# Row numbers of keys written by ScalarE, four blocks of tiles instead of three, and another order of the quantile units, in a two-layer graph kernel

## The chip, the cores and the metric

The kernel runs on one core of a Trainium2 chip. The metric is the device time of one execution in microseconds (us), the median of the runs. Engine names: PE is the matrix engine (PEld its weight loads), DVE the vector engine, ACT the scalar engine, POOL the GpSimd engine, SP the engine that only starts transfers. SBUF is the working memory of 128 partitions; PSUM is the small memory that PE writes. DRAM is the chip's large memory.

## The reference, cut to what matters

`x` is 4096 nodes by 128 numbers, `adj` a 4096 by 4096 matrix of zeros and ones with about 32 ones in a row (11 to 55 in this input). Two layers follow each other:

```python
# layer 0: graph attention with 8 heads over the neighbours of each node
Wh = einsum('nd,hde->hne', nodes, W)
e  = leaky_relu(f1[:, :, None] + f2[:, None, :], 0.2)
att = softmax(where(adj > 0, e, -9e15))
cat = elu(einsum('hnm,hmd->hnd', att, Wh)) as (N, H*D)
x1  = layernorm(nodes + elu(cat @ W1 + b1))
# layer 1: drop some neighbours of each row, then for each column
# the 0.25, 0.5 and 0.75 quantile of the kept neighbours' x1
keep = mask & ~((rank + 1) % skip == 0)
svals = sort(where(keep, x1[neighbour], big))
agg   = mean over q of svals[ceil(q * n_keep) - 1]
out   = (0.5 * agg + 0.5 * x1) @ W.T + b + x1
```

Rows with few neighbours make both layers sparse: the kernel works on lists of neighbours.

## The kernel before, in words

A *tile* is 128 nodes; there are 32. The work has three stages, and each engine runs its instructions in the order in which the program emits them (`manual_schedule(engines=ORDERED)` for PE, DVE, ACT and POOL; only SP's transfers are ordered by the compiler).

**Search** (`neighbours`). For each tile, ACT reads half a row block of `adj` (`adj_t`, 1 MB) and writes its signs as bf16 (`sgn`, L645). For each of 8 chunks of 512 columns, PE makes a *key* in PSUM in two matmuls: L684 multiplies `sgn` by 8192 times the identity (start of the sum), and L687 adds the column's number, counted down from 4096, from two constant rows (`parts`). DVE takes the 8 largest keys of each 128 columns (L651, four of them per chunk), and then eight passes of L656 and L658 over those pick the neighbours of the tile before. Keys lie in a pool `key_ps` of two PSUM buffers. One chunk of this is a *piece*; `pieces_of(n)` counts them. `complete_records` (L724 to L759) makes the lists final, and `rank_by_count` ranks the nodes of a block by their number of neighbours, so that a tile of the attention holds nodes with lists of like length. POOL scatters the records in that order (`rec_d`, L228).

**Attention** (`step`, `fetch_rows`, `attend`). The tiles are split into `BLOCKS = [6, 10, 16]`: block b is searched while block b - 1 is attended, and the first block is searched before any attention, with the node products of `node_rows` in between. `CAPS` and `LAYERS` give how many list places a tile of a block has; each place costs one gather of 128 rows (L219, `G<-xt_d,idx`), 1124 in all. A `step` fetches tile i on POOL, runs the first part of `attend` on tile i - 1 and the second part on tile i - 2, and strews a quota of search pieces between them. Gathered rows lie in 6 buffers `G` of 16 places, which come free when PE's matmuls L1015 (`y<-wide,G`) have read them. Four PSUM tiles serve the attention: `small` (sums `den`, and the output `o` of L1046), `rz`, `y` and `hT`. The last tile of a block waits for the ranks: its gathers are mixed with the record scatters of the next block. During the last block records go out once more for all nodes (`all_d`), and `lists_of_layer_1` makes the lists of layer 1.

**Quantiles** (`quantile_out`). The 32 tiles are now ranked over all nodes and form 21 units, eleven of them pairs of tiles: `[0]`, `[1]`, `[2, 3]` ... `[22, 23]`, `[24]` ... `[31]`, the last with the longest lists (62 gathers; `[0]` and `[1]` have 22 each). POOL gathers a unit's rows into `vals`, a pool of two buffers (L219, `vals<-x_d,idx`); DVE runs a selection network on it (`tensor_tensor` minimum and maximum, L1228). Between these `turn_of_gpsimd` puts a tiny copy (L1199, `junk<-still`) whenever 1.1 us or more of them have run. PE and ACT then form the output (L1246 to L1273), and POOL scatters it (`out_dram`, L228). The order was `[0]`, `[24]` ... `[31]`, the pairs from the last to the first, `[1]`. The emitted order on POOL is: the fetches of the first two units, and then for each further unit its fetch, followed by the output scatter of the unit two before it. A fetch into `vals` has to wait until the network of the unit two before it has read that buffer.

If a bound on the lists were broken, a flag would start a general path (`general_attention`, `general_quantiles`) behind the three stages.

Of the kernel before, what the change touches and what calls it, by code (L numbers as in the profile page):

```python
# [9 lines left out]
F32 = mybir.dt.float32  # L10
# [9 lines left out]
P = 128  # L20
# [12 lines left out]
MARK = 8192.0  # L33
ROUNDS = L // 8
GROUP = 4
STEPS = 24
KEEP_MIN = 6.0
FMAX = 30.0
# [3 lines left out]


CAPS = {
    6: [28, 30, 33, 35, 39, 61],
    10: [26, 28, 30, 31, 33, 34, 36, 38, 40, 61],
    16: [24, 26, 28, 29, 30, 31, 31, 32, 33, 34, 35, 36, 38, 39, 42, 62],
    32: [
        23, 24, 25, 26, 27, 27, 28, 29, 29, 30, 30, 30, 31, 31, 32, 32,
        33, 33, 34, 34, 35, 35, 36, 36, 37, 37, 38, 39, 40, 41, 44, 63,  # L50
    ],
}
BLOCKS = [6, 10, 16]


LAYERS = {
    (6, 0): [(0, 16, 0), (16, 8, 0), (24, 4, 1)],
    (6, 2): [(0, 32, 0), (32, 8, 7)],
    (6, 5): [(0, 32, 0), (32, 16, 0), (48, 16, 15)],
    (10, 0): [(0, 16, 0), (16, 8, 0), (24, 4, 2)],  # L60
    (10, 4): [(0, 32, 0), (32, 32, 31)],
    (10, 7): [(0, 32, 0), (32, 4, 0), (36, 4, 2)],
    (10, 9): [(0, 32, 0), (32, 16, 0), (48, 16, 14)],
    (16, 14): [(0, 32, 0), (32, 8, 0), (40, 4, 2)],
    (16, 15): [(0, 32, 0), (32, 16, 0), (48, 16, 14)],
}


TURNS = {6: range(6), 10: range(10), 16: [0, 1, 2, 3, 15, 4, 5, 6, *range(8, 15), 7]}

CAP = CAPS[NT]
LOW = [
# [6 lines left out]
for _u in UNITS:  # L79
    for _t in _u:  # L80
        HT[_t] = max((CAP[t] - 1) // 2 for t in _u)
LMAX = 2 * max(HT)
SLOTS = max(2 * HT[u[0]] * len(u) for u in UNITS)


# [157 lines left out]
def kernel(  # L243
# [48 lines left out]
    before = rp.tile([P, P], BF16, name="before")  # L292
    adjp = tc.alloc_tile_pool(name="adjp", bufs=2, side="right")
    cp = tc.alloc_tile_pool(name="cnt", bufs=2, side="right")
    kp = tc.alloc_tile_pool(name="key_ps", bufs=2, space=PSUM)
    parts = [adjp.tile([64, n], BF16, name=f"parts{n}", bufs=1) for n in (N // 8, 7 * N // 8)]
    markb = adjp.tile([P, P], BF16, name="markb", bufs=1)
    rowi = adjp.tile([P, P], F32, name="rowi", bufs=1)

    def search(t0, n):  # L300
        return neighbours(
            tc, adjp, cp, kp, rec, num, adj, t0, n, parts, markb, oneb, bad, jp1, pidx
        )

    with tc.tile_pool(name="setup", bufs=1) as sp, tc.tile_pool(
        name="setup_ps", bufs=2, space=PSUM
    ) as pp, tc.manual_schedule(engines=ORDERED):

        for v in parts:
            nc.vector.memset(v, 0.0)  # L310
        nc.vector.memset(oneb, 1.0)
        for v, base in zip(parts, (N, N - N // 8)):
            n = v.shape[1] // 64
            iota(nc, v[0:1, :], [[-64, n], [0, 64]], base=base)
            iota(nc, v[32:33, :], [[0, n], [-1, 64]])
        nc.vector.tensor_scalar(markb, ident, MARK, None, ALU.mult)
        iota(nc, pidx, [[0, 1]], cm=1)
        iota(nc, jp1, [[1, L]], base=1)
        nc.gpsimd.iota(
            rec.bitcast(I32)[:, :, R_OWN], pattern=[[P, NT]], base=0, channel_multiplier=1  # L320
        )
        iota(nc, rowi, [[1, P]])
        rows = node_rows(tc, sp, pp, rec, x, W, W_sb, a1, a2, Wl, wa, WlT, ident, bad, xt_d)
        for i, _ in enumerate(search(0, BLOCKS[0])):
            if i > 0:
                next(rows, None)
        for _ in rows:
            pass
        nc.vector.tensor_scalar(before, rowi, pidx, None, ALU.is_gt)
        nc.sync.dma_start(W1_sb, W1.rearrange("(h e) o -> e h o", e=P))  # L330
        for i, v in enumerate((b1, gamma, beta, bl)):
            nc.sync.dma_start(vecs[:, i, :], v.partition_broadcast(P))
        for i, big in enumerate((-BIG, BIG)):
            fill = sp.tile([P, D], F32, name=f"fill{i}")
            nc.gpsimd.memset(fill, big)
            nc.sync.dma_start(x1_d[N + i * P : N + (i + 1) * P, :], fill)
# [5 lines left out]

    weigh, store, tail = [], [], []
    consts = {}
    consts["small"] = pp.tile([P, 512], F32, name="small")

    narrow = {
        w: attp.tile([P, 32 // w, NARROW[w]], F32, name=f"narrow{w}", bufs=1) for w in NARROW
# [145 lines left out]


    pairs = [u for u in UNITS if len(u) == 2]
    order = UNITS[:1] + UNITS[2 + len(pairs) :] + pairs[::-1] + UNITS[1:2]
    with tc.tile_pool(name="sort", bufs=2) as sp, tc.tile_pool(name="fin", bufs=3) as fp, tc.tile_pool(
        name="fin_ps", bufs=2, space=PSUM
    ) as pp, tc.manual_schedule(engines=ORDERED):  # L500
        halfid = sp.tile([P, P], F32, name="halfid", bufs=1)
        nc.scalar.mul(halfid, ident, 0.5)
        still = pp.tile([P, 1], F32, name="still", bufs=1)
        nc.vector.memset(still, 0.0)
        late = dict(ident=ident, halfid=halfid, ones=ones, WlT=WlT, bl_b=vecs[:, 3, :], still=still)

        def fetch_unit(unit):
            n, k = 2 * HT[unit[0]], len(unit)
            vals = sp.tile([P, SLOTS * D], F32, name="vals")
            xs = fp.tile([P, 2, D], F32, name="xs")  # L510
            for j in range(n):
                for u, t in enumerate(unit):
                    a = (j * k + u) * D
                    gather(nc, vals[:, a : a + D], x1_d, idx[:, t, j : j + 1])
            for u, t in enumerate(unit):
                gather(nc, xs[:, u, :], x1_d, own_i[:, t : t + 1])
            return unit, vals, xs

        def write_out(unit, o):
            for u, t in enumerate(unit):  # L520
                scatter(nc, out, o[:, u, :], own_i[:, t : t + 1])

        fetched = fetch_unit(order[0])
        done = None
        for nxt in order[1:] + [None]:
            now = fetched
            if nxt:
                fetched = fetch_unit(nxt)
            if done:
                write_out(*done)  # L530
            done = quantile_out(tc, sp, fp, pp, *now, wt, late)
        write_out(*done)
    keep.release()

# [89 lines left out]
    return ROUNDS * (n + 1) + 3 * len(groups_of(n))  # L624


def neighbours(tc, adjp, cp, kp, rec, num, adj, t0, n, parts, markb, oneb, bad, jp1, pidx):


    nc = tc.nc  # L630
# [30 lines left out]
    for t in range(t0, t0 + n):  # L661
        cnt = adjp.tile([P, 2], F32, name="cnt", bufs=20)
        todo += [(t, 0, cnt), (t, 1, cnt)]
        counts[t] = cnt
    for _ in range(3):
        load()
    sign()
    late = None
    start = t0
    for t in range(t0, t0 + n + 1):  # L670

        if t < t0 + n:
            first = adjp.tile([P, NCH * 8], F32, name="first")
            firsts.append(first)
        for r in range(ROUNDS):
            done = late
            late = None
            if t < t0 + n:
                b = r % (ROUNDS // 2)
                if b == 0:  # L680
                    sgn = signs.pop(0)

                key = kp.tile([P, 512], F32, name="key")
                nc.tensor.matmul(  # L684
                    key, lhsT=markb, rhs=sgn[:, ts(b, 512)], start=True, stop=False
                )
                nc.tensor.matmul(  # L687
                    key, lhsT=oneb[0:64, :], rhs=parts[1][:, ts(r - 1, 512)] if r else parts[0], start=False, stop=True
                )
                late = (key, first, r * 512)  # L690
                if b == 0:
                    sign()
            if done:
                eights(*done)
            if t > t0:
                best(firsts[-2 if t < t0 + n else -1], t - 1, r)
            yield
        if t > t0:
            u = t - 1
            cnt = counts[u]  # L700
            nc.vector.tensor_tensor(num[:, u : u + 1], cnt[:, 0:1], cnt[:, 1:2], ALU.add)
            nc.vector.tensor_scalar(rec[:, u, 0:L], rec[:, u, 0:L], -MARK, 0.0, ALU.add, ALU.max)
            if t - t0 in groups_of(n):
                yield from complete_records(tc, cp, rec, num, bad, jp1, pidx, start, t - start)
                start = t
# [232 lines left out]
def attend(tc, ap, pp, fetched, consts):  # L938
# [20 lines left out]
    nc.scalar.activation(zs, zs, AF.Exp)  # L959
    yield  # L960

    small = consts["small"]
    den = small[:, 0 : 32 * H]
    for i, (w, g0, runs, f1v) in enumerate(parts):
        k = P // w
        for r in range(k // 4):
# [9 lines left out]
    rden = ap.tile([4, 32 * H], F32, name="rden", bufs=1)  # L976
    nc.vector.tensor_scalar(rden, den[0:4, :], TINY, None, ALU.max)
    nc.vector.reciprocal(rden, rden)  # L978
    rz = pp.tile([P, L * H], F32, name="rz")
    for i, (w, g0, runs, f1v) in enumerate(parts):  # L980
        k = P // w
        for r in range(k // 4):
# [58 lines left out]
    yield  # L1041
    nc.vector.tensor_scalar(hf, hf, 1.0, -1.0, ALU.min, ALU.add)
    nc.vector.tensor_tensor(hf, hT, hf, ALU.max)  # L1043
    o = small[:, 32 * H : 32 * H + D]
    for h in range(H):
        nc.tensor.matmul(  # L1046
            o, lhsT=hv[:, h, :], rhs=consts["W1_sb"][:, h, :], start=(h == 0), stop=(h == H - 1)
# [120 lines left out]
    nc.vector.tensor_copy(total, tot)  # L1168


def quantile_out(tc, sp, fp, pp, unit, vals, xs, wt, late):

    nc = tc.nc
    k = len(unit)
# [26 lines left out]
    for r, (d, mins, maxs) in enumerate(network):  # L1201
        after = list(where)
        for low, slots, op in ((0, mins, ALU.min), (d, maxs, ALU.max)):
# [4 lines left out]
            for (_, _, at), same in kinds.items():  # L1208
# [5 lines left out]
                parts = list(parts)  # L1214
                while parts:
                    i, c, s, m = parts.pop(0)
                    if then(c * m) > TURN_MAX:
                        room = int((TURN_AIM - then(0)) / (size * TT_EACH))
                        if ran and room < 1:
                            turn_of_gpsimd()  # L1220
# [11 lines left out]
                        op,  # L1232
                    )
                    ran = then(c * m)
                    if ran > TURN_MIN:
                        turn_of_gpsimd()
                        ran = 0.0
                for i in same:
# [262 lines left out]
```

## Time and profile before

| what | value |
|---|---|
| median of 3 runs | 3558.73 us (3556.36 to 3559.92) |
| the profiled execution's own time | 3561.78 us |
| its span in the profile | 3560.0 us |
| busy: PE, DVE, ACT, POOL | 1257.6, 2700.2, 403.2, 2510.0 us |
| first attention gather starts | 137.69 us |
| last attention gather starts | 1768.53 us |
| first quantile gather starts | 1818.31 us |
| last quantile gather starts (`xs`) | 3481.76 us |

A line of a group in the profile reads: line of the kernel, engine, operation, output and inputs, count; then busy time and mean duration of one in ns; then the engine's idle time just ahead of these instructions and what ended most of it ("issue": nothing that the profile shows). A line of the timeline reads: start, duration, engine, line, operation, and in brackets the idle time before it with what ended it. A line of waits reads: who waited, for whom, total us, times, the longest. A window line reads: from and to, its length, and for each engine the busy us and, behind an x, the number of instructions.

### The profile page before, as it was taken

To read this page: it belongs to the slowest core of one execution; us is meant where nothing else is said; L and a number is where in the kernel's file an instruction comes from. 1 tells how busy PE (TensorE), PEld (TensorE's weight loads), DVE (VectorE), ACT (ScalarE), POOL (GpSimd) and SP (SyncE) were. 2 spreads that over 40 slices of the span, in tenths; PEclk is the share of its full clock that TensorE was granted. 3 is DMA by queue.
4 is the path that set the end of the run, shared out by engine and by line. 5 is a ranking of instruction groups with operands and counts; after the bars stand their busy time and mean duration, and the time that the engine had idled before them with its cause. 6 is when DMAs were issued, how large, how long until landed. Compare 5 with 4: busy or idle time off the path is not lost. (4 is left out here: it accounts for less than half of the span.)

```text
span 3560.0 us, 22296 instructions
## 1 busy us (share of the span) xinstructions
PE 1257.6 (35%) x5323; PEld 949.8 (27%) x5323; DVE 2700.2 (76%) x7015; ACT 403.2 (11%) x579; POOL 2510.0 (71%) x2341
## 2 busy tenths in 40 slices
PE   7377568878555454555620000000000000000101
PEld 2144545555455454454520000000000000000101
DVE  8787458877435222247538999999999999999998
ACT  3122122222111111111110000000000000000000
POOL 1475767657777777777747777788777688777771
PEclk9955556555556555555555555555555555555555
DMA  6442254432222222232211111111111111111110
GB/s 232 136 150 77 67 159 131 139 119 75 59 65 54 56 53 55 54 70 55 52 30 48 47 46 46 43 43 41 44 42 46 34 40 41 41 42 41 40 42 12
DMA packets 109132, 237.42 MB, mean 67 GB/s; under 512 B 46720, under 2 KB 63104, under 8 KB 100800
## 3 DMA queue, kind: packets, MB, share of 16 engines
q0 software_dynamic: 74368, 156.34, 17.6%
q10 hardware_dynamic: 14848, 70.85, 5.8%
q1 hardware_dynamic: 19776, 8.73, 1.2%
q8 instruction: 44, 0.72, 0.1%
q14 instruction: 96, 0.79, 0.1%
HBM read 224.60 MB, written 11.15 MB: 66 GB/s over the span
## 5 line engine op out<-in xcount | busy, mean ns | idle before, releaser
L219 POOL DMA_INDIRECT vals<-x_d,idx x1024 | 1219.8, 1191 | 315.7 <-issue 308.7
L219 POOL DMA_INDIRECT G<-xt_d,idx x1124 | 1094.5, 974 | 419.9 <-issue 330.8
L1228 DVE TENSOR_TENSOR work<-work 128x512 f32<-128x512 f32 (+7 forms) x1194 | 933.7, 811 | 0.6
L1247 PE MATMUL st_ps<-dg,goal 128*128 128x128 f32 x286 | 71.4, 427 | 1605.9 <-DVE goal L1228 1605.1
L1228 DVE TENSOR_TENSOR work<-work,work 128x512 f32<-128x512 f32 (+6 forms) x821 | 590.8, 741 | 0.5
L1015 PE MATMUL y<-wide,G 128*128 128x32 f32 (+3 forms) x2248 | 485.6, 394 | 29.0 <-DVE wide L1002 28.9
L1247 PEld LDWEIGHTS st_ps<-dg,goal 128*128 128x128 f32 x286 | 63.3, 322 | 1612.3 <-issue 1611.4
L1015 PEld LDWEIGHTS y<-wide,G 128*128 128x128 f32 x2248 | 463.5, 310 | 65.4 <-DVE wide L1002 31.8
L651 DVE MAX8 first<-key 128x8 f32<-128x128 f32 x1024 | 225.2, 282 | 109.0 <-PE key L687 108.6
L952 DVE TENSOR_TENSOR z<-G,f1x 128x128 f32<-128x128 f32 (+5 forms) x92 | 28.8, 327 | 307.7 <-DMA G<-xt_d,idx 302.3
L684 PE MATMUL key<-sgn,markb 128*128 128x512 bf16 x256 | 150.5, 588 | 131.8 <-DVE first L651 87.9
L1228 DVE TENSOR_TENSOR work<-vals 128x1536 f32<-128x1536 f32 (+7 forms) x96 | 133.4, 1404 | 47.9 <-DMA vals<-x_d,idx 47.5
L1199 DVE COPY junk<-still 128x1 f32<-128x1 f32 x1118 | 168.8, 151 | 0.0
L645 ACT ACTIVATE sgn<-adj_t 128x2048 bf16<-128x2048 int32 x64 | 122.1, 1907 | 333.8 <-PE key L684 277.9
L1046 PE MATMUL small<-W_sb,late 128*128 128x128 f32 x512 | 127.3, 434 | 88.3 <-DVE late L1043 88.3
L1246 ACT ACTIVATE dg<-ident,wt 128x128 f32<-128x128 f32 x143 | 47.5, 394 | 930.9 <-PE st_ps L1247 930.6
L967 PE MATMUL small<-z,own 128*4 128x32 f32 (+6 forms) x438 | 49.3, 279 | 285.4 <-ACT z L959 285.4
L687 PE MATMUL key<-parts,oneb 64*128 64x512 bf16 x256 | 148.4, 580 | 0.5 <-POOL parts L237 0.5
L1046 PEld LDWEIGHTS small<-W_sb,late 128*128 128x128 f32 x512 | 112.8, 327 | 102.6 <-DVE late L1043 98.9
L983 PE MATMUL rz<-rden,ownT 4*128 4x32 f32 (+6 forms) x438 | 96.6, 383 | 78.6 <-DVE rden L978 63.7
L1034 PE MATMUL hT<-late,W_sb 128*128 128x128 f32 x512 | 110.2, 383 | 35.4 <-ACT late L1028 35.4
L228 POOL DMA_INDIRECT out_dram<-o,own_i x32 | 44.7, 1398 | 105.9 <-ACT o L1273 83.6
(184 smaller groups left out, 1784.4 us busy)
## 6 DMA issues: line engine op xcount, KB each, us to landing
adj_t<-in_adj_dram ACTq DMA_DIRECT2D x64, 1024.0 KB
G<-xt_d,idx POOLq DMA_INDIRECT x1124
vals<-x_d,idx POOLq DMA_INDIRECT x1024
R<-rec_d SPq DMA_DIRECT2D x128, 26.2 KB
xt_d<-rec SPq DMA_DIRECT2D x4, 544.0 KB
rec<-in_x_dram ACTq DMA_DIRECT2D x4, 512.0 KB
narrow<-rec_d SPq DMA_DIRECT2D x68, 5.2 KB
a_b<-in_L_gnn_a_dram ACTq DMA_DIRECT2D x2, 512.0 KB
```

Source lines behind the costliest of these rows:

```text
L219: nc.gpsimd.indirect_dma_start(out=dst, out_offset=None, in_=rows, in_offset=bass.IndirectOffsetOnAxis(ap=idx, axis=0),)
L645: nc.scalar.activation(sgn, adj_t, AF.Sign, accum_out=cnt[:, i : i + 1])
L651: nc.vector.max(first[:, ts(c0 // CW + c, 8)], key[:, ts(c, CW)])
L684: nc.tensor.matmul(key, lhsT=markb, rhs=sgn[:, ts(b, 512)], start=True, stop=False)
L687: nc.tensor.matmul(key, lhsT=oneb[0:64, :], rhs=parts[1][:, ts(r - 1, 512)] if r else parts[0], start=False, stop=True)
L983: nc.tensor.matmul(rz[:, layer[i] * H : (layer[i] + w - g0) * H], lhsT=ownT[w][:, r, :], rhs=rden.rearrange("p (g r h) -> p r g h", r=k // ...
L1015: nc.tensor.matmul(yf[:, ts(g, c)], lhsT=G[:, col + j - a, 0:D], rhs=pf[:, ts(j, c)], start=(i == 0 and g % (w // 2) == w // 2 - 1), stop= ...
L1034: nc.tensor.matmul(hT[:, ts(h, P)], lhsT=consts["W_sb"][:, h, :], rhs=yT[:, h, :], start=True, stop=True)
L1046: nc.tensor.matmul(o, lhsT=hv[:, h, :], rhs=consts["W1_sb"][:, h, :], start=(h == 0), stop=(h == H - 1))
L1199: nc.vector.tensor_copy(junk, late["still"])
L1228: nc.vector.tensor_tensor(slots_of(dst, (j, c, s, m), size), slots_of(a, (i, c, s, m), size), slots_of(b, (i + d, c, s, m), size), op,)
L1247: nc.tensor.matmul(st_ps[:, u, :], lhsT=goal[:, (j * k + u) * D : (j * k + u + 1) * D], rhs=dg, start=(j == 0), stop=False,)
```

## The change

It has five parts.

1. The column numbers of keys no longer come from PE. ACT writes them into the PSUM buffer (`seed`: an Identity activation of a constant row `rows` with the chunk's `base` as bias, 128x512), and the one matmul that is left adds onto them (`start=False`). A buffer's first use in a search is opened by a matmul with `start=True`. There are three key buffers instead of two, and a seed is issued two chunks ahead of its matmul. `parts` and its set-up are gone.
2. `small` is gone, which frees the PSUM bank for the third key buffer: `den` lies in `rz`, and `o` in the first 128 columns of `hT`.
3. `BLOCKS = [4, 6, 9, 13]`, with `CAPS`, `LAYERS` and `TURNS` of their own. The list places are 151 + 217 + 317 + 451 = 1136 gathers, where 217 + 351 + 556 = 1124 were.
4. The units' order is `[0]`, `[1]`, `[24]` ... `[30]`, the pairs from the last to the first, `[31]`. Units `[0]` and `[1]` share one `vals` buffer, and the fetches of the first three units stand in a row. POOL's order of fetches and output scatters keeps its form.
5. The last unit (`[31]`) runs its network without `turn_of_gpsimd` and without cutting long instructions.

```diff
+KEYS = 3
-BLOCKS = [6, 10, 16]
+BLOCKS = [4, 6, 9, 13]
...
-    kp = tc.alloc_tile_pool(name="key_ps", bufs=2, space=PSUM)
-    parts = [adjp.tile([64, n], BF16, name=f"parts{n}", bufs=1) for n in (N // 8, 7 * N // 8)]
+    kp = tc.alloc_tile_pool(name="key_ps", bufs=3, space=PSUM)
+    rows = adjp.tile([P, 512], F32, name="rows", bufs=1)
+    base = adjp.tile([P, ROUNDS], F32, name="base", bufs=1)
...
-        for v in parts:
-            nc.vector.memset(v, 0.0)
         nc.vector.memset(oneb, 1.0)
-        for v, base in zip(parts, (N, N - N // 8)):
-            n = v.shape[1] // 64
-            iota(nc, v[0:1, :], [[-64, n], [0, 64]], base=base)
-            iota(nc, v[32:33, :], [[0, n], [-1, 64]])
+        iota(nc, rows, [[-1, 512]])
+        iota(nc, base, [[-512, ROUNDS]], base=N)
...
+    def seed(r):
+        key = kp.tile([P, 512], F32, name="key")
+        if len(opened) < KEYS:
+            nc.tensor.matmul(key, lhsT=markb, rhs=signs[0][:, 0:512], start=True, stop=True)
+            opened.append(key)
+        nc.scalar.activation(key, rows, AF.Identity, bias=base[:, r : r + 1])
+        seeded.append(key)
+
     for _ in range(3):
         load()
     sign()
+    opened, seeded = [], []
+    chunks = [r for _ in range(n) for r in range(ROUNDS)]
+    for _ in range(KEYS - 1):
+        seed(chunks.pop(0))
...
-                key = kp.tile([P, 512], F32, name="key")
-                nc.tensor.matmul(
-                    key, lhsT=markb, rhs=sgn[:, ts(b, 512)], start=True, stop=False
-                )
-                nc.tensor.matmul(
-                    key, lhsT=oneb[0:64, :], rhs=parts[1][:, ts(r - 1, 512)] if r else parts[0], start=False, stop=True
-                )
+                key = seeded.pop(0)
+                nc.tensor.matmul(
+                    key,
+                    lhsT=markb,
+                    rhs=sgn[:, ts(b, 512)],
+                    start=False,
+                    stop=True,
+                    skip_group_check=True,
+                )
...
             if done:
                 eights(*done)
+            if chunks:
+                seed(chunks.pop(0))
...
-    small = consts["small"]
-    den = small[:, 0 : 32 * H]
+    rz = pp.tile([P, L * H], F32, name="rz")
+    den = rz[:, 0 : 32 * H]
...
-    o = small[:, 32 * H : 32 * H + D]
+    o = hT[:, 0:D]
...
-    order = UNITS[:1] + UNITS[2 + len(pairs) :] + pairs[::-1] + UNITS[1:2]
+    alone = UNITS[2 + len(pairs) :]
+    order = UNITS[:2] + alone[:-1] + pairs[::-1] + alone[-1:]
...
-            vals = sp.tile([P, SLOTS * D], F32, name="vals")
+            if unit is order[1]:
+                vals = shared[0][:, SHORT * D : (SHORT + n) * D]
+            else:
+                vals = sp.tile([P, SLOTS * D], F32, name="vals")
+                shared.append(vals)
...
-        fetched = fetch_unit(order[0])
+        fetched = [fetch_unit(v) for v in order[:2]]
         done = None
-        for nxt in order[1:] + [None]:
-            now = fetched
-            if nxt:
-                fetched = fetch_unit(nxt)
+        for i in range(len(order)):
             if done:
                 write_out(*done)
-            done = quantile_out(tc, sp, fp, pp, *now, wt, late)
+            if i + 2 < len(order):
+                fetched.append(fetch_unit(order[i + 2]))
+            now, last = fetched.pop(0), i == len(order) - 1
+            done = quantile_out(tc, sp, fp, pp, *now, wt, late, last)
...
-                    if then(c * m) > TURN_MAX:
+                    if not last and then(c * m) > TURN_MAX:
...
-                    if ran > TURN_MIN:
+                    if not last and ran > TURN_MIN:
                         turn_of_gpsimd()
```

## The prediction

> **What bounds the kernel now.** I read the page first (slices and costliest groups), then POOL's timeline for the ends of the stages, then the waits and windows inside the attention, then windows that count gathers and turns in the sorts.
>
> The page, the 40 slices (89 us each) and four groups:
>
> ```profile
> DVE  8787458877435222247538999999999999999998
> POOL 1475767657777777777747777788777688777771
> ...
> L219 POOL DMA_INDIRECT vals<-x_d,idx x1024 | 1219.8, 1191 | 315.7 <-issue 308.7
> L219 POOL DMA_INDIRECT G<-xt_d,idx x1124 | 1094.5, 974 | 419.9 <-issue 330.8
> ...
> L684 PE MATMUL key<-sgn,markb 128*128 128x512 bf16 x256 | 150.5, 588 | 131.8 <-DVE first L651 87.9
> ...
> L687 PE MATMUL key<-parts,oneb 64*128 64x512 bf16 x256 | 148.4, 580 | 0.5 <-POOL parts L237 0.5
> ```
>
> Three stages show. In slices 1 and 2 POOL does next to nothing while DVE searches. From 137.69 to 1769.5 us (last gather's end) POOL gathers nearly without a break: 7 tenths is full here, since a gather of 0.974 us is followed by 0.30 of issue, 1.274 in all. From slice 22 DVE sorts at 9 tenths, and POOL is near full beside it. POOL's waits from 137 to 1770 us, DVE's from 463 to 925, and all engines in that window:
>
> ```profile
> POOL G L219 <- PE y L1015: 73.3, 8, 30.0
> ...
> POOL x_d L228 <- DVE f1b L898: 7.4, 1, 7.4
> ```
>
> ```profile
> DVE first L651 <- PE key L687: 72.5, 44, 4.8
> ```
>
> ```profile
> 463.00:925.00 462.00, 369.11 (x1471) 244.52 (x1471) 354.18 (x1312) 120.36 (x128) 314.98 (x323) 0.59 0.40 117
> ```
>
> So while a block is searched the attention falls behind the gathers: POOL waits for `G` buffers (73.3 us), because DVE waits for keys (72.5 us of 462) behind a PE that is busy for 369.1 us; ACT is busy for 120.4.
>
> In the sorts, the start of the first two units and the pace of POOL (windows of units `[24]`, `[31]` and `[6, 7]`; first the gathers L219, then the turns L1199):
>
> ```profile
> 1847.17 1.83 DVE L1228 TENSOR_TENSOR work<-vals 128x768 f32<-128x768 f32 x2 [32.05 <-DMA vals<-x_d,idx]
> 1897.90 1.29 DVE L1228 TENSOR_TENSOR work<-vals 128x512 f32<-128x512 f32 x2 [15.49 <-DMA vals<-x_d,idx]
> ```
>
> ```profile
> 1897.90:1963.00 65.10, 49.76 (x47) 0.50 0.18 48
> 2395.30:2539.50 144.20, 115.06 (x92) 0.51 0.16 42
> ...
> 3293.30:3374.80 81.50, 62.91 (x49) 0.52 0.15 40
> ```
>
> ```profile
> 1897.90:1963.00 65.10, 6.86 (x46) 0.50 0.18 48
> 2395.30:2539.50 144.20, 14.41 (x96) 0.51 0.16 42
> ...
> 3293.30:3374.80 81.50, 7.62 (x51) 0.52 0.15 40
> ```
>
> 47 gathers against 46 turns, 92 against 96, 49 against 51: beside a sort POOL gets about one gather for each turn, every 1.4 to 1.6 us. That is what the new order of units has to live with.
>
> **Part 1, the first search.** One tile takes DVE 12.6 us (L701 starts at 80.13 and at 92.75), and the first block's record scatters follow each other every 2.8 us (114.80 to 128.69, five steps). Two tiles fewer: 25.2 + 5.6, and about 1 for shorter ranks: 32 us, first gather at 106. Three covers. ACT: per tile two signs of 2.1 with 0.7 of transfer issue, eight copies of 0.26, two of 0.21, and eight seeds. A seed's price lies between copies from PSUM of 128x256 (0.37 us) and the Exp of 128x1024 (1.02); by their slope 0.59, so 4.7 in all. The sum, 12.1, still lies under DVE's 12.6; at 1.02 a seed ACT would take 15.5 and cost 3 us a tile, 12 in all. `node_rows` gets 42 search pieces to hide behind where it had 61, so some ten of its steps run after them, 0.55 us each (copies at 61.10, 61.63, 62.17) on PE and ACT; they hide behind DVE's last eight-passes (9.8 us from 92.86 on), and cost 6 if not. The opening matmuls are 12 of 0.59 us on PE, which waits anyway.
>
> **Part 2, POOL's work in the attention.** Before: 1124 x 1.274 = 1432, 86 scatters between the gathers at about 1.3 = 112, and pauses. POOL's timeline gives pauses of 22.3, 8.0 and 30.0 us in the steps, and 18.0 and 6.8 around the two block changes (lists must land, and a tile of 49 or 50 places takes four buffers): 85 in all. 1432 + 112 + 85 = 1629; it took 1631.8. After: 1136 x 1.274 = 1447 (+15), 88 scatters (two more record scatters) = 114, and the same rest of 3: 106 + 1564 = 1670 plus pauses. Three block changes at 12.4 (mean of the two): 37.
>
> **Part 3, the pauses in the steps.** Before, 60.3 us over 14 steps with search pieces (5 + 9), 4.3 each. Now there are 3 + 5 + 8 = 16 steps, with as much search in each (6/3, 9/5, 13/8 tiles against 10/5, 16/9). A step of the second block took 462/9 = 51 us, in which PE was busy 41 and DVE waited 8.1 for keys. With 14.2 chunks a step PE loses 14.2 x 0.54 (two keys start 0.54 apart) = 7.7 us, and a third buffer lets it run one chunk (1.6 us of DVE) further ahead. Bounds: all 8.1 go, a step (43) is shorter than the fetch of a tile (36 gathers, 47 us), and no pause is left; or nothing goes, because the seed of 0.59 stands in the chain from DVE's read to the next key where L687's 0.54 stood, and ACT in its order may hold it behind a sign (2.1), the copy L1028 (1.88) and table loads (1.28): 16 x 4.3 = 69. Only the matmuls' share is sure, so I take half, 4 us a step; as the fetch then sets the pace of some steps, 1.8 of pause is left: 29. Last gather at 1670 + 37 + 29 = 1736, **34 us earlier** (63 earlier with no pause, 6 later with all). The way from there to the first quantile gather (48.8 us) holds one tile's attention, unchanged. `den` in `rz` and `o` in `hT` wait for reads of the tile before that DVE has long done; nothing.
>
> **Part 4, the order of units.** At the start nothing is won: `[0]` sorts for 35.2 us while the next fetch took 50.7 (the 15.5 of idle above). Now `[0]` and `[1]` sort for 35.2 + 32.1 while two fetches (23 + 37 transfers at 1.37) take 82: idle 15 again. The end is what changes. Before, POOL took 1664 us from 1818.3 to its last fetch, 21 of them idle (6.5 and 14.8, waiting for an output): 1643 of work, 92 gathers of it during `[31]`'s 144.2 us. As `[31]` now sorts last, all fetches must be done before that sort begins. Their work is the same 1643, less about 12, since some 40 gathers run at 1.24 beside an idle DVE instead of 1.5: 1631 after the first gather. DVE alone would be there earlier: 29 + 35 + 32 + 15 + 1472 (its sorts from 1897.9 to 3546.5 without `[31]` and `[1]`) = 1583. So DVE waits 48 us more; adding the fetches and sorts up unit by unit puts 35 of them ahead of `[31]`, the rest ahead of the last pairs.
>
> **Part 5, the last unit without turns.** 96 turns of 0.07 us (start to start) go: 144 becomes 137. 1631 + 137 = 1768 against 1728 before (3546.5 less 1818.3): 40 later. Behind the sort PE has 14 targets instead of 4, and about nine matmul pairs of 0.5 us come after the last minimum instead of four: 3 more. With 1 for the landing, **44 us later**. Bounds: at 3% off the pace of the gathers, 20 to 70; if POOL kept up, 4 earlier (7 less 3).
>
> **Sum.** 3561.8 (the profiled execution) - 34 + 44 = 3572; the median lay 3 under that execution: **3569 us**.
>
> **A rule against part 1.** No row of before has ACT writing into a buffer that PE then adds to. The Trainium skill, "PSUM — Partial Sum Buffer", section "The four PSUM rules", says that ScalarE's writes neither set nor clear the bits that make a matmul add, and that a seed other than 0 is safe only where an earlier matmul left the bit set. By it the opening matmuls are what makes the seeds count, and without them every list would be wrong; the sum would then be the general path's, not mine.
>
> **Rivals.** (a) *Key waits vanish*: no pauses, -63 + 44 = -19, 3540, faster. It decides when a step gets shorter than a tile's fetch, 47 us. For it: PE's 369 of 462. Against: the waits on PE's own chains stay. 0.22. (b) *The fetches keep up*: -34 - 4, 3521. Against: one gather a turn in every window. 0.08. (c) *ACT takes PE's place* in the chain: +6 + 44, 3609. 0.15. (d) *The seeds don't add*: lists wrong, the flag starts the general path, thousands of us. 0.02. My forecast: 0.53, by itself 3552 to 3586.
>
> **How the numbers follow.** This kernel can be told from no change at about 0.2%, 7 us. Of the forecast 0.31 lies above, 0.15 within, 0.07 below; (a) gives 0.20 and 0.02, (b) 0.08 below, (c) and (d) 0.17 above. Rounded: faster 0.34, same 0.17, slower 0.49. The range reaches from (a)'s to near (c)'s time: 3536 to 3604.
>
> **What would show it.** First gather at 106; DVE's waits for keys under 4.5 us a step; last `G` gather near 1736; idle of DVE ahead of `[31]`'s first L1228 about 35 us, with POOL gathering `vals` back to back until then. Wrong, if `[31]` starts without a wait, or if the `G` waits for `y` are above 70 or near 0.

## The result, and the profile after

The changed kernel takes 3552.7 us (median of 20 runs, 3548.4 to 3558.9), the kernel before 3557.9 in as many. The ratio is 0.9986 (95% interval 0.9979 to 0.9993): some 5 us faster, where the forecast was 10 slower. The profiled execution took 3552.89 us with a span of 3551.1. The span of before is 8.9 longer; that execution lay 3.9 above the median of its kernel.

The page of the changed kernel, the slices of DVE and POOL and five groups:

```profile
DVE  7683883688823521376478999999999999999878
POOL 0676777676776777777477777777787877877720
...
L228 POOL DMA_INDIRECT vals<-x_d,idx x1024 | 1209.0, 1181 | 316.0 <-issue 301.4
L228 POOL DMA_INDIRECT G<-xt_d,idx x1136 | 1110.0, 977 | 389.4 <-issue 320.0
...
L664 DVE MAX8 first<-key 128x8 f32<-128x128 f32 x1024 | 223.8, 281 | 71.9 <-PE key L710 71.1
L684 ACT ACTIVATE key<-rows,base 128x512 f32<-128x512 f32 x256 | 174.2, 687 | 316.4 <-DVE first L664 257.5
...
L710 PE MATMUL key<-sgn,markb 128*128 128x512 bf16 x256 | 140.7, 575 | 121.4 <-ACT key L684 120.7
```

POOL stands at 6 and 7 in the second and third slices, where it began with 4 and 7, and at the other end it falls to 2 and 0 while DVE still sorts. One matmul a key is left on PE, and what PE now waits for is the seed. In the waits of the attention (POOL from 109 to 1723 us, DVE from 109 to 1200) the two waits that the forecast was about are both about half of what they were; DVE's is 106.8 us in the same window of the kernel before (the last line).

```profile
POOL G L228 <- PE y L1044: 42.0, 10, 10.6
...
POOL G L228 <- DVE f1b L928: 4.5, 1, 4.5
```

```profile
DVE first L664 <- PE key L710: 55.1, 31, 5.3
```

```profile
DVE first L651 <- PE key L687: 106.8, 67, 5.8
```

In the sorts, DVE's timeline at the first instructions of `[24]` and of `[31]`, and windows of the sort of `[24]` (gathers L228, then turns L1228) and of the idle stretch ahead of `[31]`:

```profile
1884.11 1.29 DVE L1257 TENSOR_TENSOR work<-vals 128x512 f32<-128x512 f32 x2 [17.46 <-DMA vals<-x_d,idx]
...
3397.19 4.16 DVE L1257 TENSOR_TENSOR work<-vals 128x3840 f32<-128x3840 f32 x1 [33.62 <-DMA vals<-x_d,idx]
```

```profile
1884.10:1949.30 65.20, 48.92 (x46) 0.50 0.16 48
...
3363.50:3397.20 33.70, 25.34 (x27) 0.55 0.17 53
```

```profile
1884.10:1949.30 65.20, 6.89 (x46) 0.50 0.16 48
```

46 gathers beside 46 turns, as before; 27 gathers in 33.7 us (one every 1.25) while DVE stands still. So the last unit waits for rows, by 33.6 us where 35 were forecast.

The span, cut where the forecast cut it:

| from the traces, us | before | after | moved | forecast |
|---|---|---|---|---|
| first attention gather | 137.7 | 109.2 | -28.5 | -32 |
| POOL between first and last gather, without pauses | 1547 | 1567 | +20 | +17 |
| pauses at block changes | 25 | 31 | +6 | +12 |
| pauses in the steps | 60 | 15 | -45 | -31 |
| last attention gather's end | 1769.5 | 1722.2 | **-47** | -34 |
| from there to the first quantile gather | 48.8 | 48.1 | -1 | 0 |
| from there to the end of the last sort | 1728.2 | 1764.6 | **+36** | +40 |
| from there to the end of the span | 13.5 | 16.3 | +3 | +4 |

The pauses after are the gaps of POOL's transfers: 5.5, 2.2 and 7.5 in the steps; 7.7, then 3.2 and 7.3, then 1.9 and 10.6 around the three block changes. The table keeps the forecast's cut, but one pause of before stands in the wrong row:

```profile
854.58 0.97 POOL L219 DMA_INDIRECT G<-xt_d,idx  x1 [5.22 <-PE y L1015]
```

The forecast counted these 5.2 us at the second block change. They stand 72 us ahead of the first record scatter of that change (927.0), among steps that still search; a pause of 6.9 at the same place of e4 below is counted with the steps. By place, before has 65 us in the steps and 20 at the changes, and the moves are -50 and +11. The sum is the same.

### The profile page after: what moved, and what is told of

It reads as the page before. It is cut to its first block, busy times and chain, and to the rows that moved or that the text cites. A ratio compares the mean times of both kernels' runs of the same rounds, so it can differ in the third digit from the quotient of the medians.

```text
span 3551.1 us, 22542 instructions
## 1 busy us (share of the span) xinstructions
PE 1133.1 (32%) x5230; PEld 968.7 (27%) x5230; DVE 2706.5 (76%) x7004; ACT 567.9 (16%) x835; POOL 2503.0 (70%) x2351
## 5 line engine op out<-in xcount | busy, mean ns | idle before, releaser
L228 POOL DMA_INDIRECT vals<-x_d,idx x1024 | 1209.0, 1181 | 316.0 <-issue 301.4
L228 POOL DMA_INDIRECT G<-xt_d,idx x1136 | 1110.0, 977 | 389.4 <-issue 320.0
L1257 DVE TENSOR_TENSOR work<-work 128x512 f32<-128x512 f32 (+8 forms) x1189 | 929.7, 812 | 0.8
L1044 PEld LDWEIGHTS y<-wide,G 128*128 128x128 f32 x2272 | 480.9, 314 | 71.9 <-DVE wide L1031 48.0
L684 ACT ACTIVATE key<-rows,base 128x512 f32<-128x512 f32 x256 | 174.2, 687 | 316.4 <-DVE first L664 257.5
L982 DVE TENSOR_TENSOR z<-G,f1x 128x128 f32<-128x128 f32 (+4 forms) x97 | 29.0, 318 | 226.6 <-DMA G<-xt_d,idx 225.0
L1228 DVE COPY junk<-still 128x1 f32<-128x1 f32 x1022 | 151.8, 149 | 0.0
L1075 PE MATMUL hT<-W_sb,late 128*128 128x128 f32 x512 | 124.5, 429 | 77.1 <-DVE late L1072 77.1
L1012 PE MATMUL rz<-rden,ownT 4*128 4x32 f32 (+6 forms) x500 | 112.2, 386 | 111.7 <-DVE rden L1008 98.6
L1075 PEld LDWEIGHTS hT<-W_sb,late 128*128 128x128 f32 x512 | 114.2, 327 | 91.3 <-DVE late L1072 88.9
L1012 PEld LDWEIGHTS rz<-rden,ownT 4*128 4x128 f32 x500 | 101.6, 294 | 127.4 <-DVE rden L1008 110.4
L997 PE MATMUL rz<-z,own 128*4 128x32 f32 (+6 forms) x500 | 55.2, 280 | 241.6 <-ACT z L989 241.4
```

What stands on the lines that cost most here:

```text
L228: nc.gpsimd.indirect_dma_start(out=dst, out_offset=None, in_=rows, in_offset=bass.IndirectOffsetOnAxis(ap=idx, axis=0),)
L684: nc.scalar.activation(key, rows, AF.Identity, bias=base[:, r : r + 1])
L997: nc.tensor.matmul(den[0:4, :].rearrange("p (g r h) -> p r g h", r=k // 4, h=H)[:, r, g0:], lhsT=own[w][:, ts(r, 4)], rhs=z[:, layer[i] : ...
L1012: nc.tensor.matmul(rz[:, layer[i] * H : (layer[i] + w - g0) * H], lhsT=ownT[w][:, r, :], rhs=rden.rearrange("p (g r h) -> p r g h", r=k // ...
L1044: nc.tensor.matmul(yf[:, ts(g, c)], lhsT=G[:, col + j - a, 0:D], rhs=pf[:, ts(j, c)], start=(i == 0 and g % (w // 2) == w // 2 - 1), stop= ...
L1075: nc.tensor.matmul(o, lhsT=hv[:, h, :], rhs=consts["W1_sb"][:, h, :], start=(h == 0), stop=(h == H - 1))
```

## The experiments

The theory after the result: three terms that add up, about -45 from the keys (parts 1 and 2), 0 from the blocks, +39 from the order of the units. Rivals: that the blocks brought the gain, that the end was late for another reason than the order, and, inside the keys, that a buffer and not the relief of PE was what counted. Each run below is compared with the kernel before on the same chip (3557.5 to 3560.6 us); the changed kernel's 0.9986 is the mark for edits of it.

**e1_old_order: keys and blocks, without the new order.**

```diff
-    order = UNITS[:2] + alone[:-1] + pairs[::-1] + alone[-1:]
+    order = UNITS[:1] + UNITS[2 + len(pairs) :] + pairs[::-1] + UNITS[1:2]
...
-                    if not last and ran > TURN_MIN:
+                    if ran > TURN_MIN:
```

> The changed kernel with parts 4 and 5 undone: the units in the old order, [1] last, each with its turns, two fetches ahead; keys and blocks as changed. Theory (three terms that add up: keys about -45 us, blocks about 0, order of units about +39): the end gets 39 us earlier than in the changed kernel, 3514 us, 44 under the kernel before; the last sort ends some 1728 us after the first quantile gather, as in the kernel before, and no unit in the middle waits over 5 us for its rows. Rival (the loss at the end is not the order's, but a slower pace of the gathers after the new attention): about 3553, as the changed kernel.

3514.9 us, ratio 0.9878 (0.9863 to 0.9893): 38 under the changed kernel. The last sort ends 1728.7 us after the first quantile gather. DVE's waits for rows, which were 84.0 us in the changed kernel, are those of the start alone (32.6 and 15.6):

```profile
L1248 DVE TENSOR_TENSOR work<-vals 128x1536 f32<-128x1536 f32 (+7 forms) x96 | 133.4, 1406 | 48.6 <-DMA vals<-x_d,idx 48.2
```

**e2_new_order: the new order and the last unit without turns, on the kernel before** (the diff of parts 4 and 5).

> The kernel before with parts 4 and 5 alone: new order of units, the last one without turns; keys and blocks as before. Theory: +39 us, about 3597, with 30 to 35 us of idle of DVE ahead of the sort of [31], while POOL gathers. Rival (the stage costs 39 only behind the changed attention): within 10 us of 3558.

3595.7 us, 1.0107 (1.0092 to 1.0122). The same wait stands ahead of `[31]` in its timeline, behind an attention that is as it was:

```profile
3440.84 8.23 DVE L1237 TENSOR_TENSOR work<-vals 128x3840 f32<-128x3840 f32 x2 [33.74 <-DMA vals<-x_d,idx]
```

By the ratios both runs give the order the same price, 38 us, with either attention: the loss at the end is the order's.

**e3_keys_alone: parts 1 and 2 on the kernel before**, and **e4_blocks_alone: part 3 on it** (the diffs of those parts).

> The kernel before with parts 1 and 2 alone: seeds by ACT, one matmul a key, three key buffers; three blocks, old order of units. Theory: the pauses of POOL in the steps fall from 60 us to about 15, and the time by 45: 3513 us; first attention gather where it was, near 138; waits of DVE for keys in the second block's window fall from 72 us to under 50. The step on record (half of the key wait goes) would give 31 less, 3527. Rival (the blocks brought the gain, the keys little): 3540 or more.

> The kernel before with part 3 alone: blocks of 4, 6, 9 and 13 tiles, keys by two matmuls as before, old order of units. Theory: 28 us won in the first search, 17 lost to twelve more places and two more record scatters, 6 to 12 lost at the third block change, pauses in the steps as before with two steps more (0 to 9): -5 to +10, 3553 to 3568 us. Rival (the blocks brought the gain): 28 or more less, 3530 or under.

Keys alone: 3519.6 us, 0.9889 (0.9874 to 0.9904). Blocks alone: 3561.3 us, 1.0003 (0.9994 to 1.0012). The gain is the keys', and four blocks give nothing by themselves; on top of the keys they give 5 us at most (e1's 3514.9 against 3519.6, with intervals that overlap). The waits from 109 to 1200 us, keys alone and then blocks alone:

```profile
DVE first L648 <- PE key L694: 54.7, 26, 5.3
...
POOL G L220 <- PE y L1028: 15.6, 7, 10.0
```

```profile
DVE first L658 <- PE key L694: 108.2, 75, 5.8
POOL G L226 <- PE y L1022: 90.0, 10, 22.0
```

Keys alone take the pauses in the steps from 65 to 19 us (10.0 and 9.3). With blocks alone those pauses are 55 (22.0, 13.7, 12.3, 6.9), so in the new blocks the keys take away 40: 55 to 15. Blocks alone bring the first gather to 103.1, 35 earlier; keys alone move it from 137.7 to 145.5, 8 later. 103.1 plus 6 is the changed kernel's 109.2. That loss was not in the forecast, and it led to e8.

**e5_two_buffers and e6_third_buffer: what of the keys it is.** The changed kernel with `KEYS = 2` and two buffers; and with three buffers, but the pair of matmuls in place of the seed:

```diff
-KEYS = 3
+KEYS = 2
-    kp = tc.alloc_tile_pool(name="key_ps", bufs=3, space=PSUM)
+    kp = tc.alloc_tile_pool(name="key_ps", bufs=2, space=PSUM)
```

```diff
-                key = seeded.pop(0)
+                key = kp.tile([P, 512], F32, name="key")
                 nc.tensor.matmul(
...
-                    start=False,
-                    stop=True,
-                    skip_group_check=True,
-                )
+                    start=True, stop=False
+                )
+                nc.tensor.matmul(
+                    key, lhsT=oneb[0:64, :], rhs=parts[1][:, ts(r - 1, 512)] if r else parts[0], start=False, stop=True
+                )
```

> The changed kernel with two key buffers instead of three, so that a seed is issued one chunk ahead; seeds still by ACT and one matmul a key. Theory A (the relief of PE brings the 40 us of shorter pauses): within 10 us of the changed kernel's 3553. Theory B (the third buffer brings it): 40 us or more above it, 3593 or more. The step on record took half of the key wait for both together; half each would give 3573.

> The changed kernel with its three key buffers, but with keys made by PE alone in two matmuls as before; blocks and order of units as changed. Theory A (relief of PE): 30 to 40 us above the changed kernel, less the 6 us of later first keys, so 3577 to 3587. Theory B (buffer): within 10 us of 3547, and perhaps under the changed kernel, since the first search starts 6 us earlier.

Two buffers: 3569.7 us, 1.0026 (1.0017 to 1.0035), 14 to 17 above the changed kernel. Third buffer without seeds: 3600.2 us, 1.0106 (1.0090 to 1.0122), what the new order costs by itself (e2), so the third buffer brings nothing where PE makes the keys in two matmuls. Waits from 109 to 1200 us, e5 and then e6:

```profile
DVE first L664 <- PE key L710: 74.8, 49, 5.3
POOL G L228 <- PE y L1044: 53.3, 10, 13.2
```

```profile
DVE first L666 <- PE key L702: 108.8, 74, 5.8
POOL G L227 <- PE y L1029: 93.5, 10, 23.2
```

108.8 us of key waits with three buffers are the 108.2 of e4 with two, although PE itself waits half as long for DVE to free a buffer (e4, then e6). That speaks for PE's own time as what is short:

```profile
PE key L691 <- DVE first L658: 72.6, 38, 26.6
```

```profile
PE key L699 <- DVE first L666: 37.4, 18, 26.1
```

The sharing of `rz` and `hT` (part 2) is in e6 too, and costs nothing there that shows. Theory A was right on e6, though the price was 13 above the upper end of its range; on e5 its range ended 7 below. Out of some 45 us, about 30 are the relief of PE, and about 15 the third buffer, which counts only with seeds. PE's wait for seeds, with two buffers and then with three, shows what it covers:

```profile
PE key L710 <- ACT key L684: 168.5, 78, 25.1
```

```profile
PE key L710 <- ACT key L684: 88.3, 40, 25.4
```

Of POOL's pauses alone (99 us in e6, 56 in e5, 46 in the changed kernel) the relief of PE takes four fifths; 4 of the third buffer's 15 us lie in the first search (first gather at 113.5 against 109.2).

**e7_seed_twice: twice the seeds.**

```diff
         nc.scalar.activation(key, rows, AF.Identity, bias=base[:, r : r + 1])
+        nc.scalar.activation(key, rows, AF.Identity, bias=base[:, r : r + 1])
```

> The changed kernel with each seed written twice in a row: 256 more ACT instructions of 0.69 us, 176 us in all. Theory (seeds lie under DVE's work, ACT has room at 568 us busy of 3551): at most 15 us more, 3568 or less. Rival (c) of the prediction (a seed stands in the chain from DVE's read to the next key): 0.69 us for a good part of the 224 chunks after the first block, 60 us or more, 3613 or more.

3579.5 us, 1.0051 (1.0037 to 1.0065): 23 to 27 more, between the two: the theory's 15 did not hold either. In its trace the last attention gather ends 30 later, of which 13 stand in the first search (first gather at 122.0) and 6 in pauses (52 instead of 46). The other 11 are nearly all the gathers' own time, the mean of one going from 977 to 986 ns (the other runs here have 974 to 981); why, no run tells. Rival (c) is refuted in the attention: twice the seeds lengthen the pauses by 6 us, and DVE's key waits from 55.1 to 67.9. ACT is close to the bound in the first search only, where 32 seeds more (22 us) cost 13.

**e8_load_late: what holds the seeds at the start.** ACT's timeline from 6 to 18 us in the changed kernel:

```profile
6.08 1.91 ACT L658 ACTIVATE sgn<-adj_t 128x2048 bf16<-128x2048 int32 x1 [2.63 <-DMA adj_t<-in_adj_dram]
...
13.17 0.35 ACTq L651 DMA_DIRECT2D adj_t<-in_adj_dram  x1
13.62 1.30 ACT L684 ACTIVATE key<-rows,base 128x512 f32<-128x512 f32 x2 [5.54 <-DMA vecs<-in_L_gnn_gamma_dram]
```

The first seed does not wait for `rows`, nor for PE's opening matmul, which was over at 9.1. It stands behind the issue of a transfer of `adj`, and that waits for a small transfer of SP's (`vecs`) whose semaphore it shares in the built program. In the kernel before the same issue has no such wait; the changed set-up has other assignments of semaphores:

```profile
7.98 0.33 ACTq L638 DMA_DIRECT2D adj_t<-in_adj_dram  x1
```

The edit issues that transfer, and the next, after the fifth seed (`hold` leaves a transfer out of `sign`):

```diff
-    def sign():
+    def sign(hold=False):
...
-            load()
+            if not hold:
+                load()
...
-    sign()
+    sign(t0 == 0)
...
-                    sign()
+                    sign(t0 == 0 and t == 0 and r == 0)
+                if t0 == 0 and t == 0 and r == 3:
+                    load()
+                    load()
```

> The changed kernel with one order changed on ACT: in the first tile of the first search the two transfers of adj that follow the first two signs are issued after the fifth seed instead of ahead of the first and the third, since the first of them waits some 5 us on ACT for a transfer of SP's to land, and the seeds wait behind it. Theory: first MAX8 of a key near 10.4 instead of 15.0, first attention gather near 104 instead of 109.2, time 5 us less, 3548. Rival (the seeds' 0.69 us make the first search longer): the same 109 and 3553.

3547.7 us, 0.9962 (0.9949 to 0.9976): 5 less than the changed kernel by the medians, 8 by the ratios. The seeds start with the opening matmul:

```profile
8.90 1.30 ACT L685 ACTIVATE key<-rows,base 128x512 f32<-128x512 f32 x2 [0.74 <-PE key L683]
```

The first MAX8 of a key is at 10.3, the first gather at 105.2. Two to three us above e4's 103.1 and e6's 102.3 stay, and may be the seeds' own. So most of the loss in the first search was the wait, not the price of a seed.

**e9_turns_in_last: the last unit with its turns.**

```diff
-            done = quantile_out(tc, sp, fp, pp, *now, wt, late, last)
+            done = quantile_out(tc, sp, fp, pp, *now, wt, late, False)
```

> The changed kernel with the turns of the last unit kept: [31] runs with its 96 copies and its cuts. Theory: the sort of [31] takes 144 us instead of 137.7, and nothing else moves: 6 to 7 us more than the changed kernel, 3559. Rival (turns cost nothing, since they overlap): 3553.

3557.3 us, 0.9998 (0.9989 to 1.0007): 4 to 5 more, less than the 6 to 7 of the theory. Its timeline shows where the rest is:

```profile
3380.09 1.89 DVE L1257 TENSOR_TENSOR work<-vals 128x1664 f32<-128x1664 f32 x1 [12.43 <-DMA vals<-x_d,idx]
3397.24 1.89 DVE L1257 TENSOR_TENSOR work<-vals 128x1664 f32<-128x1664 f32 x1 [15.18 <-DMA vals<-x_d,idx]
3402.80 1.83 DVE L1257 TENSOR_TENSOR work<-vals 128x512 f32<-128x512 f32 x2 [3.61 <-DMA vals<-x_d,idx]
```

The cut pieces of the first instruction need fewer rows, so two of them run while the rest of the rows is still on its way: 144.2 less twice 1.89 are 140.4 after the last wait, where the uncut sort takes 137.7. Part 5 took the cuts away with the turns.

**e10_long_early and e11_old_late: versions that beat both.** Both have the late transfer of e8. e10 moves `[31]` ahead of the pairs and leaves `[0]` and `[1]` first; e11 has the old order with all turns.

```diff
-    order = UNITS[:2] + alone[:-1] + pairs[::-1] + alone[-1:]
+    order = UNITS[:2] + alone + pairs[::-1]
```

> The changed kernel with the late transfer of the run before, and one change in the order of units: [0], [1], [24] ... [31], the pairs, so that [2, 3] sorts last, without turns. Theory (the loss is that the 62-place unit sorts when nothing is left to fetch, not the three fetches in a row): the idle ahead of [31] goes, the last sort ends some 1724 us after the first quantile gather instead of 1764; time 3505 to 3512. Rival (the three fetches in a row and [0], [1] first cost too): 3520 or more.

> The changed keys and blocks, the late transfer of the first search, and the old order of units with all turns: the sum of two gains found one by one, 3515 for the order and 5 to 8 for the transfer. Theory: they add up, 3507 to 3510. Rival (the earlier start is taken up by a longer pause later in the attention): 3513 or more.

e10: 3516.5 us, 0.9884 (0.9869 to 0.9899). The idle ahead of `[31]` is gone, and the last sort ends 1728.0 after the first quantile gather: moving the 62-place unit alone takes 37 us off this stage, and `[0]` and `[1]` in front, with three fetches in a row, win nothing over the old order's 1728. It misses its range by 4 us: the start idles 17.6 instead of 15.6, the last pair is only 2.6 faster without turns, and 19.6 us come after its sort where `[1]` has 14.4. e11: **3510.3 us, 0.9871** (0.9856 to 0.9886), 47 under the kernel before. In its trace the first gather and the end of the span are each 4 us earlier than in e1, so there the transfer's gain is kept; the times say 5 less than e1 by the medians and 2 by the ratios, too close to tell whether the two gains add up in full. It is the best version here.

## Why the prediction was wrong

The mechanisms were the right ones, and the sum of two large terms of opposite sign was off by more than what it came to: -34 and +44 forecast, -48 and +39 found. The time lies in the range of 3536 to 3604, but on the other side of no change.

**Part 3 holds the error.** The step that failed is the pauses' term: means of the old blocks were carried over to more steps of shorter blocks, "16 x 4.3 = 69" and "three block changes at 12.4 (mean of the two): 37". That is 106 us before the keys help, and e4, with the old keys, shows 96. The split behind the two means was off as well. With the pause of 854.6 us in its place the old blocks had 4.7 a step and 9.8 a change, which would give 75 and 29; e4 has 55 and 41 (16.9, 5.0, 6.8, 1.8, 10.6). None of the 55 stands in the three steps of e4's first block, where the mean put 13; the first is at 510 us. What makes a pause fall in one step and not in another, no run tells.

The other step, half of the key waits going, held in the steps: forecast 69 to 29, 40 away; measured 55 to 15, 40 away. DVE waited 106.8 / 14 = 7.6 us a step for keys and now 55.1 / 16 = 3.4 (under the 4.5 of the forecast). But the keys shorten the pauses at the block changes too, from 41 (e4) to 31, which the forecast put at nothing. So the pauses came to 46 where 29 + 37 = 66 stood: 10 by the means, 10 by the changes. The 3 of part 1 and 3 of POOL's work go against them.

**Why half goes** was argued by two things, PE's matmuls and the third buffer. e5 and e6 part them: in time two thirds are PE's matmuls and one third the third buffer, which is nothing without seeds.

**Part 1.** Two tiles fewer gave 35 (e4) where 32 were forecast. That ACT's seeds lie hidden in the first search was wrong by 6 us, but not for the reason that the bounds allowed: 0.687 us a seed, in the bounds of 0.37 to 1.02, cost 2 to 3 at most, and the wait of a transfer's issue ahead of the seeds the rest (e8). The step "ACT per tile: two signs of 2.1 with 0.7 of transfer issue" counted what the issue takes and not what it waits for.

**Part 4** was right in kind and nearly in size: 33.6 us ahead of `[31]` (35 forecast), POOL gathering back to back until then, the last pairs held for 6.3 more. In all 40 of waiting instead of 48, since the rows were there 1627 us after the first gather, not 1631, and DVE alone would have needed 1587, not 1583. The idle at the start, 15 forecast, was 17.5. The bounds of 20 to 70 were too narrow for the 3% that they name: 3% of 1631 us is 49, not 25. And the gathers beside a sort came every 1.4 to 1.7 us (81.5 us for 49 of them beside `[6, 7]`), where the forecast read 1.4 to 1.6. **Part 5**: 137.7 (137), and 2.8 behind the sort (3). The 7 us of the turns were no gain of 7: 4 to 5 by e9.

**The rivals.** (a), all pauses gone, is refuted by the 15 us left, though the time came nearer to its 3540 than to the forecast's 3569. (b) is refuted by the 33.6 us ahead of `[31]`, (c) by e7, and (d) by the time itself: the general path did not start. The seeds count, as the rule of the Trainium skill ("PSUM — Partial Sum Buffer", "The four PSUM rules") has it for a buffer that a matmul opened; no run here left those matmuls out.

With e4's 96 us of pauses in place of 106, and the 40 that the keys take as they were, the forecast would have been 10 lower, 3559: no change, by its own bound of 7 us. With the 10 at the block changes too it would have been 3549, faster; the measured 3552.7 lies between.

## What to carry to other kernels

When a forecast is the difference of two terms several times its size, look first at the mean that was carried over to another shape, here pauses per step and per block change: 10 us of error there were the whole of the forecast's 10, and 10 more, a relief counted at nothing, turned the sign. Where the last stage overlaps fetching with computing, put the unit with the longest computation where there is still something to fetch behind it, and a short one last: that order alone is worth 1% here. And when work moves to another engine, read what stands ahead of it in that engine's order, transfers' issues included: an issue of 0.35 us held ACT for 5.

## What the runs showed that was not expected

- An engine's transfer issue can wait for another engine's transfer: ACT stood from 8.1 to 13.2 us for a transfer that SP had started, and e8 took the wait away by order alone.
- Writing 128x512 f32 from SBUF into PSUM took ACT 687 ns (256 of them), above the 590 that the forecast's line through a PSUM copy and an Exp gave. The Trainium skill, "ScalarE: Activation LUTs", section "What ACT_TABLE_LOAD costs", gives 280 ns and 0.833 ns an element for an activation with a bias column; 706 ns is the estimate by it, and the measured 687 is near.
- A third PSUM buffer of keys is worth 14 to 17 us behind ACT's seeds and nothing behind PE's pair of matmuls (e5, e6).
- Twice the seeds made POOL's gathers 1% longer (977 to 986 ns), with no wait that the profile names.
